# A graph-convolution and state-space kernel: the preparation of an item moved one slot up, and sums over channels taken by full products

## The chip, the cores and the metric

The kernel runs on one core of a Trainium2 chip. The core has a matmul engine (PE, with its weight loads shown apart as PEld), a vector engine (DVE), an activation engine (ACT), a general engine (POOL) and queues that issue DMA transfers (SP's is used here). The engines run side by side, each takes its own instructions strictly in the order of the program, and semaphores hold an instruction until its data and buffers are free. The metric is the device time of one execution in microseconds; the median of three runs counts.

## The reference, cut to what matters

The input is 16 images of 96 channels and 64 x 64 pixels. The first layer works in windows of 8 x 8 pixels: it finds each pixel's 9 nearest pixels of the window (by normalised channels), mixes pairs of pixels and takes the maximum. The second layer normalises each pixel over its channels and runs a state recurrence along the 4096 pixels, twice.

```python
# layer 0, per window of 64 pixels
y = affine(conv1x1(x, fc1_w, fc1_b), fc1_s, fc1_t)
xn = nodes / maximum(norm(nodes, axis=-1), 1e-12)          # sum of squares over 96 channels
idx = top_k(-(sq - 2 * xn @ xn.T + sq.T), 9)
h = max over k of gelu(affine(concat(x_i, x_j - x_i) @ ew + eb))
x = affine(conv1x1(h, fc2_w, fc2_b), fc2_s, fc2_t) + x
# layer 1, twice per image
h = (seq - mu) * rsqrt(var + 1e-5) * ln_g + ln_b           # mean and variance over 96 channels
xs, z = split(h @ in_w)
xc = silu(causal 4-tap convolution of xs)
dt, B, C = split(xc @ xproj_w)                             # 6, 16, 16 columns
delta = softplus(dt @ dt_w + dt_b)
state = exp(delta * A) * state + delta * B * xc            # 192 channels x 16 states
y = (sum over states of state * C + Dp * xc) * silu(z)
seq = seq + y @ out_w
```

At the end come a 1 x 1 convolution with a pooled term, a batch norm over all images and the residual.

## The kernel before, in words

**Rows and items.** The 4096 pixels of an image are 8 rows of windows, each 512 pixels. The first layer is done row by row: `nearest` (L288) finds the neighbours, `edges` (L360) the mixed pairs. The second layer is done in items (image, layer, row): 256 items, `n` from 0 to 255. Layer is `i` (0 or 1), row is `k`.

**Slots.** The main loop (L741) has one slot for each item `n` and each pair of states `p` from 0 to 7: 2048 slots, eight to an item. In a slot, for each of three blocks of 128 x 512, DVE makes `db` = u * B (`times_b`, L648) and runs the recurrence as a scan (L789). B comes from PE: `bcast` (L643) spreads two rows of `dbl` over 128 partitions into the PSUM tile `bt`, of which there is one buffer only. `bt` of the next slot is emitted in this slot, right after this slot's `db`s, and is read by the next slot's first `db`, which DVE takes ahead of this slot's third scan (L788). POOL multiplies the scans by C (`ct`, L803) and PE sums the products over the states (`folded`, L651: `ya` and `yb`); the sum of slot m - 1 is emitted at the end of slot m, behind everything else PE has in slot m, except in slot 0, where the sum of the old item's slot 7 comes ahead of it. ACT makes the decays `da` = exp(delta * A) for the slot after next (`chosen`, L626, called by `ahead`).

**Work between.** All other work is written as generators, each yielding once a slot. The loop keeps them in the list `going` and advances each by one step per slot, in the order of the list, between the first and the second scan. These are:

- `norm` (L509): the normalisation of an item; its sum over channels is `by_pixel` (L271): four products with one column each, 128 pixels per product.
- `prelude` (L540): the convolution and `z` with their silu (L567), then dt, B and C (`pd`, `dbl`), softplus (L590 to L613, ACT and POOL), and 16 DMAs that lay out delta and u.
- `nearest`: fc1, square, `by_pixel`, power, a trip through DRAM, scores, the eight largest, the indices to DRAM.
- `edges`: two halves; in each the indices come back, ACT makes one-hots (L384, L385), PE `pv` and ACT `vu`, then PE `t` and ACT gelu (L412); DVE takes maxima (L415, queued in `later`, and run between scans); `pf2` (L462) and the update of the row (L474).
- `tail` (L670): the out-projection of the item before, and for layer 1 the fusion product `po` and its statistics.

In the code's time, before the change, the steps of `prelude` for item n + 2 fall in slots 5, 6, (7), 0, 1, 2, 3, 4; `norm` for n + 3 in slots 7 to 4; gelu in slots 2 and 3; `tail` begins in slot 4. `nearest` and `edges` of a row begin in slot 5 of an odd item, so a row takes two items.

**PSUM.** All products of the generators share one ring `pm` of two buffers (tag `mm`): a product waits until the one two before it has been read. A step whose result DVE reads is split by `apart`: its products are emitted at the end of the steps of this slot (`close_steps`) and DVE's read at the start of the next slot's steps (`open_steps`).

**Tables.** Gelu and silu need another activation table than exp and ln. A generator that yields `TABLE` holds the loop off from calling `ahead` before the next slot's steps (`held`), so that the exps come after the burst.

Of the kernel before, what the change touches and what calls it, by code (L numbers as in the profile page):

```python
# [20 lines left out]
def tile_conv_knn_mamba(ctx: ExitStack, tc: tile.TileContext, w: dict, out: bass.AP):  # L21
# [107 lines left out]
    fc2_b, fc2_s, fc2_t = (column(f"fc2_{k}", f"L0_conv_fc2_{k}") for k in "bst")  # L129
    srow = load("fc2_srow", [128, C], w["L0_conv_fc2_s"].unsqueeze(0).to_broadcast([128, C]))  # L130
    nc.vector.tensor_tensor(fc2T, fc2T, srow.unsqueeze(1).to_broadcast([128, 3, C]), ALU.mult)

# [21 lines left out]
    )  # L154
    ones_c = const.tile([C, 1], F32, name="ones_c")
    nc.vector.memset(ones_c, 1.0)
    mhalf = const.tile([128, QJ], F32, name="mhalf")
# [87 lines left out]
    between = deque()  # L245
    later = []
    NDA = 12
# [19 lines left out]
    def open_steps():  # L267
        while opening:
            opening.pop(0)()

    def by_pixel(src, name):  # L271

        ps = pm.tile([128, QJ], F32, tag="mm", name=name)
        for j in range(QJ):
            nc.tensor.matmul(  # L275
                ps[:, j : j + 1],
                lhsT=src.rearrange("c (p j) -> c j p", j=QJ)[:, j, :],
                rhs=ones_c,
                start=True,
                stop=True,  # L280
            )
        return ps

# [4 lines left out]
    def nearest(b, q):  # L288
# [20 lines left out]
        nc.gpsimd.tensor_tensor(sq, y, y, ALU.mult)  # L309
        yield  # L310
        r4 = pr.tile([128, 2, QJ], F32, tag="r4", name=f"r4_{nm}")

        def clamped(ps):
            nc.vector.tensor_scalar(r4[:, 0], ps, 1e-24, None, ALU.max)
            nc.vector.tensor_copy(r4[:, 1], ps)

        apart(partial(by_pixel, sq, f"ss_{nm}"), clamped)
        yield

        nc.gpsimd.tensor_tensor(r4[:, 0], r4[:, 0], mhalf, ALU.pow)  # L320
        nc.gpsimd.tensor_tensor(r4[:, 1], r4[:, 1], r4[:, 0], ALU.mult)
# [7 lines left out]
        nc.sync.dma_start(out=hs[NN : NN + 1].rearrange("o w j -> o (w j)"), in_=r4_d[1:2, :])  # L329
        yield  # L330
        yield
# [28 lines left out]
    def edges(b, q):  # L360
# [3 lines left out]
        idx_d = chosen_of.pop((b, q))  # L364


        hqa = pr.tile([128, Q], F32, tag="hqa", name=f"hqa_{nm}", bufs=1)
        hqb = pr.tile([128, QH], F32, tag="hqb", name=f"hqb_{nm}", bufs=1)
        hqa4 = hqa.rearrange("p (r w c) -> p w r c", r=WS, w=NW)
        hqb4 = hqb.rearrange("p (r w c) -> p w r c", r=WS, w=NP)  # L370
        for hf in range(2):
# [4 lines left out]
            )  # L376
            yield
            yield
            vus = []
            for p in range(2):  # L380
                oh = ohs[p]

                ohj = oh[0:NN].rearrange("j w i k -> j w (i k)")
                nc.scalar.activation(ohj, idb[:, 2 * p : 2 * p + 2, :], AF.Abs, bias=minus_node)  # L384
                nc.scalar.activation(ohj, ohj, AF.Relu, bias=1.0, scale=-1.0)  # L385

                pv = pm.tile([128, 2, O], F32, tag="mm", name=f"pv_{nm}_{hf}_{p}")
                for h in range(2):
                    nodes = y[:, bass.ts(4 * hf + 2 * p + h, NN)]
                    nc.tensor.matmul(pv[0:NN, h, :], lhsT=nodes, rhs=ew2, start=True, stop=True)  # L390
                    nc.tensor.matmul(pv[NN:128, h, :], lhsT=nodes, rhs=ewd, start=True, stop=True)
                vu = pr.tile([128, 2, O], F32, tag="vu", name=f"vu_{nm}_{hf}_{p}")
                nc.scalar.copy(vu, pv)  # L393
                vus.append(vu)
                yield
            yield


            for p in range(2):
                ohw = [ohs[p][:, h].rearrange("j i k -> j (i k)") for h in range(2)]  # L400
                for part in range(3):
# [3 lines left out]
                    else:  # L405
# [7 lines left out]
                    w2 = 2 * hf + p  # L413
                    later.append(
                        partial(  # L415
# [34 lines left out]
            yield  # L450
            if hf == 0:
                yield
        yield
        yield
        nc.vector.tensor_tensor(hqa, hqa, sa, ALU.max)
        nc.vector.tensor_tensor(hqb, hqb, sb, ALU.max)
        yield
# [51 lines left out]
    def norm(n):  # L509

        b, i, k = items[n]
        nm = f"{b}_{i}_{k}"
        seq = seqs[b, k]
        hn = hns[n % NHN]
        if k == 0:
            nc.gpsimd.memset(hn[:, :HALO], 0.0)
        else:
            nc.gpsimd.tensor_copy(hn[:, :HALO], hns[(n - 1) % NHN][:, Q:])
        pc = pm.tile([C, Q], F32, tag="mm", name=f"pc_{nm}")
        nc.tensor.matmul(pc, lhsT=cmat, rhs=seq, start=True, stop=True)  # L520
        sq = pr.tile([C, Q], F32, tag="sq", name=f"sqv_{nm}")
        nc.scalar.activation(sq, pc, AF.Square)  # L522
        yield
        v4 = pr.tile([128, QJ], F32, tag="v4", name=f"v4_{nm}")
        apart(
            partial(by_pixel, sq, f"pvar_{nm}"),
            lambda ps: nc.vector.tensor_scalar(v4, ps, 1.0 / C, EPS, ALU.mult, ALU.add),
        )
        yield
        nc.gpsimd.tensor_tensor(v4, v4, mhalf, ALU.pow)  # L530
        yield
        rs_d = dram.tile([128, QJ], F32, tag="rs_d", name=f"rsd_{nm}")
        nc.sync.dma_start(out=rs_d, in_=v4)
        rs = pr.tile([C, Q], F32, tag="rs", name=f"rs_{nm}")
        nc.sync.dma_start(out=rs, in_=rs_d.rearrange("p j -> (p j)").unsqueeze(0).to_broadcast([C, Q]))
        yield
        yield
        nc.gpsimd.tensor_tensor(hn[:C, HALO:], seq, rs, ALU.mult)  # L538

    def prelude(n):  # L540
# [5 lines left out]
        xc = pr.tile([128, Q + QH], F32, tag="xc", name=f"xc_{nm}")  # L546
        z = pr.tile([128, Q + QH], F32, tag="z", name=f"z_{nm}", bufs=3)

# [26 lines left out]
        yield  # L575
        yield
        dbl = dbls[n % 2]
# [21 lines left out]
        for v, cols in ((va, slice(0, Q)), (vb, slice(Q, Q + QH))):  # L599
            nc.scalar.activation(e[:, cols], v, AF.Abs)  # L600
            nc.scalar.activation(rl[:, cols], v, AF.Relu)
        nc.scalar.activation(e, e, AF.Exp, scale=-1.0)
        s1 = pr.tile([128, Q + QH], F32, tag="s1", name=f"s1_{nm}", bufs=1)
# [47 lines left out]
    def folded(n, p, hb, y):  # L651

        i = items[n][1]
        xc = made[n][0]
        if p == 3:
            nc.tensor.matmul(y[0], lhsT=dp_diag[i][:, 0, :], rhs=xc[:, :Q], start=False, stop=False)
            nc.tensor.matmul(y[1], lhsT=dp_diag[i][:, 1, :], rhs=xc[:, Q:], start=False, stop=False)
        for h in range(2):
            nc.tensor.matmul(y[0][half(h)], lhsT=fold, rhs=hb[:, h, :], start=(p == 0), stop=(p == NPR - 1))  # L659
        for h in range(2):  # L660
            nc.tensor.matmul(  # L661
                y[1][half(h)], lhsT=fold, rhs=hb[:, 2, bass.ts(h, QH)], start=(p == 0), stop=(p == NPR - 1)
            )
# [6 lines left out]
    def tail(n):  # L670
# [17 lines left out]
        if i == NL - 1:  # L688
            yield
            yield  # L690
            yield
            po = pm.tile([C, Q], F32, tag="mm", name=f"po_{nm}")
            nc.tensor.matmul(po, lhsT=fusT[:, 0, :], rhs=seq, start=True, stop=True)
            o = pr.tile([C, Q], F32, tag="o", name=f"o_{nm}", bufs=1)
            nc.scalar.activation(o, po, AF.Identity, bias=gcs[b])
            yield
            nc.vector.bn_stats(stats[:, b * NQ + k, :], o)
            nc.sync.dma_start(out=o_d[b][:, bass.ts(k, Q)], in_=o)

    def drain(*several):  # L700

        several = list(several)
        while several:
            open_steps()
            several = [g for g in several if next(g, several) is not several]
            close_steps()
            while later:
                later.pop(0)()
        open_steps()
# [5 lines left out]
    for q in range(NQ):  # L715
        drain(*([nearest(0, q + 1)] if q + 1 < NQ else []), edges(0, q))
    for n in range(3):
        drain(norm(n))
        if n < 2:
            drain(prelude(n))  # L720

    AHEAD = 2
    order = [(n, p) for n in range(NI) for p in range(NPR)]
    coming = deque(order)
# [16 lines left out]
    for m, (n, p) in enumerate(order):  # L741
# [7 lines left out]
        if n > 1 and n % 2 == 1 and p == 5 and edge_row < NB * NQ:  # L749
            going.append(edges(*divmod(edge_row, NQ)))  # L750
            edge_row += 1
        between.extend(later)
        later.clear()
        if p == 0 and k == 0:
            state = pr.tile([128, NPR, NB3], F32, tag="state", name=f"state_{nm}")
        if p == 0 and i == 0 and k == 4:
            going.append(pooled(b))
        if p == 7 and n + 3 < NI:
            going.insert(0, norm(n + 3))
        if p == 5 and n + 2 < NI:  # L760
            going.insert(0, prelude(n + 2))
        ct, das = soon.pop((n, p))
# [6 lines left out]
        for c in range(NB3):  # L769
            if c == 1:  # L770
                if p == 1 and n:
                    gate(n - 1, y)
                if p == 4 and n:
                    going.append(tail(n - 1))
                open_steps()
                if not held:
                    ahead()
# [14 lines left out]
            if between and p not in (0, 1):  # L792
                between.popleft()()  # L793
        if p and behind is not None:
            if p == 1:
# [64 lines left out]
```

## Time and profile before

| | us |
|---|---|
| median of 3 runs (lowest, highest) | 14888.06 (14887.3, 14892.01) |
| the profiled execution's own time | 14897.12 |
| its span, first to last instruction | 14895.3 |
| setup, first image's rows, first items' preparation | up to 511 |
| main loop | 511 to 14611 |
| batch norm and output | 14614 to 14895 |

| engine | busy us | share of the span |
|---|---|---|
| PE | 13574.3 | 91% |
| DVE | 13114.8 | 88% |
| POOL | 10278.8 | 69% |
| ACT | 10114.4 | 68% |

| group | count | mean ns |
|---|---|---|
| scan L789, DVE | 6144 | 1269 and 1209 |
| `db` L648, DVE | 6144 | 680 |
| `hb` times C L803, POOL | 2048 | 3450 |
| `da` L637, ACT | 6144 | 710 |
| one-column products L275, PE | 3072 | 372 |
| their weight loads L275, PEld | 3072 | 327 to 330 |
| one-hots L384 and L385, ACT | 512 each | 1146 and 1057 |
| softplus L602, L604, L606, L607, ACT | 256 each | 845, 843, 844, 935 |
| power L530, POOL | 256 | 1018 |
| `rs` from DRAM, DMA | 256 | 3.4 us from issue to landing |
| table loads, ACT | 1024 | 1283 |

A profile is one execution. Busy time of PE is modelled from pipelined matmuls, so that a PE at 91% is not a PE at its peak; a matmul in fp32 appears as two instructions. The granted clock (PEclk) is the share of TensorE's full clock that its throttle let through; over the span it is 0.891. A row of a group gives shape, count, busy time, the mean of one and, behind the last bar, how long the engine sat idle before these instructions and what ended it.

### The profile page before, as it was taken

Reading aid. Unit: us, or ns where it says so; the run is one execution under the profiler, and the core shown is the slowest. Engines: PE = TensorE matmul, PEld = TensorE weight load, DVE = VectorE, ACT = ScalarE, POOL = GpSimd, SP = SyncE. Lnnn points to the kernel's source line nnn. Section 1 sums busy time; section 2 is a strip of 40 time slices with the busy share of each in tenths; the row PEclk is TensorE's granted clock in tenths of the full one; section 3 lists DMA queues with packets and bytes.
Section 4 is the critical chain, followed back from the end, with each engine's and each line's share of the span. In section 5 each row is a group of like instructions: output and inputs, shape, how many; then the busy total and the mean of one; then the engine's idle time right before and its main releaser. Section 6 shows DMA issues by size and latency. Waiting matters only on the chain. (4 is left out here: it accounts for less than half of the span.)

```text
span 14895.3 us, 168323 instructions
## 1 busy us (share of the span) xinstructions
PE 13574.3 (91%) x50248; PEld 5491.6 (37%) x50248; DVE 13114.8 (88%) x17401; ACT 10114.4 (68%) x14517; POOL 10278.8 (69%) x6279
## 2 busy tenths in 40 slices
PE   5799999999999999999999999999999999999982
PEld 2233333333333333333333333333333333333330
DVE  2699999999998999999999999999999999999984
ACT  4477777777777777777777777777777677677652
POOL 0577777777777777777777777777777777777771
PEclk8799899989998999999999999999999999989885
DMA  1233333333333333333333333333333333333337
GB/s 27 61 82 86 83 82 83 84 83 81 86 84 79 85 84 83 80 85 85 81 84 84 83 81 86 84 80 85 83 83 82 84 86 80 85 83 82 81 81 218
DMA packets 934023, 1256.95 MB, mean 84 GB/s; under 512 B 304672, under 2 KB 436142, under 8 KB 923888
## 3 DMA queue, kind: packets, MB, share of 16 engines
q1 hardware_dynamic: 929520, 1221.01, 31.7%
q10 hardware_dynamic: 3584, 25.17, 0.4%
q8 instruction: 396, 6.49, 0.2%
q14 instruction: 523, 4.28, 0.1%
HBM read 756.89 MB, written 85.98 MB: 57 GB/s over the span
## 5 line engine op out<-in xcount | busy, mean ns | idle before, releaser
L803 POOL TENSOR_TENSOR hb<-hb,ct 128x1536 f32<-128x1536 f32 x2048 | 7065.1, 3450 | 678.1 <-DVE hb L789 187.2
L789 DVE TENSOR_TENSOR_SCAN hb<-da,state,db 128x512 f32<-128x512 f32 x5376 | 6781.1, 1269 | 0.0
L648 DVE TENSOR_TENSOR db<-u,bt 128x512 f32<-128x512 f32 x6144 | 3992.1, 680 | 672.4 <-PE bt L643 670.3
L637 ACT ACTIVATE da<-delta,a 128x512 f32<-128x512 f32 x6144 | 3900.5, 710 | 61.6 <-DVE hb L789 48.6
L643 PE MATMUL bt<-dbl,bsel 39*128 39x512 f32 x4096 | 2466.0, 683 | 333.6 <-DVE db L648 330.3
L659 PE MATMUL ya<-hb,fold 128*64 128x512 f32 x8192 | 2424.8, 673 | 89.4 <-POOL hb L803 89.1
L802 POOL COPY state<-hb 128x3 f32<-128x3 f32 x1792 | 337.8, 189 | 2975.2 <-DVE hb L789 2550.8
L412 ACT ACTIVATE g<-t,eb,es 128x512 f32<-128x512 f32 x1536 | 1184.8, 777 | 1015.8 <-PE t L404 728.1
L567 ACT ACTIVATE xc<-pj,conv_b 128x512 f32<-128x512 f32 (+1 forms) x512 | 297.4, 581 | 1959.6 <-PE pj L555 1018.8
L661 PE MATMUL yb<-hb,fold 128*64 128x256 f32 x8192 | 1368.8, 415 | 0.0
L404 PE MATMUL t<-oh,vu 128*128 128x512 f32 x2048 | 1176.1, 700 | 45.7 <-ACT vu L393 29.4
L661 PEld LDWEIGHTS yb<-hb,fold 128*64 128x64 f32 x8192 | 640.5, 150 | 1359.0 <-issue 1358.7
L643 PEld LDWEIGHTS bt<-dbl,bsel 39*128 39x128 f32 x4096 | 659.4, 201 | 1164.1 <-DVE db L648 634.7
L555 PE MATMUL pj<-hn,conv_in 97*128 97x512 f32 x2048 | 953.0, 608 | 27.9 <-POOL hn L538 27.9
L789 DVE TENSOR_TENSOR_SCAN hb<-da,db 128x512 f32<-128x512 f32 x768 | 922.6, 1209 | 0.0
L659 PEld LDWEIGHTS ya<-hb,fold 128*64 128x64 f32 x8192 | 503.6, 145 | 1070.4 <-issue 726.9
L407 PE MATMUL t<-oh,vu 128*64 128x512 f32 x2048 | 583.7, 649 | 214.2 <-ACT g L412 209.2
L584 ACT COPY dbl<-pd 38x512 f32<-38x512 f32 x256 | 148.3, 579 | 855.9 <-PE pd L581 855.9
L404 PEld LDWEIGHTS t<-oh,vu 128*128 128x128 f32 x2048 | 386.2, 211 | 801.4 <-issue 521.4
L793 DVE TENSOR_REDUCE hqa<-g 128x64 f32<-128x512 f32 x960 | 634.1, 661 | 0.4 <-ACT g L412 0.3
L390 PE MATMUL pv<-ewT,y 96*64 96x192 f32 x2048 | 478.1, 361 | 124.7 <-ACT sqv L522 124.4
L384 ACT ACTIVATE oh<-idb,minus_node 64x1024 f32<-64x1024 uint16 x512 | 586.9, 1146 | 6.7 <-DMA idb<-idxd 6.7
(160 smaller groups left out, 18671.8 us busy)
## 6 DMA issues: line engine op xcount, KB each, us to landing
ct<-cd SPq DMA_DIRECT2D x4096, 128.0 KB, 3.0
delta<-ln SPq DMA_DIRECT2D x1024, 128.0 KB, 2.4
u<-s SPq DMA_DIRECT2D x1024, 128.0 KB, 2.3
idb<-idxd SPq DMA_DIRECT2D x256, 256.0 KB, 4.0
delta<-ln SPq DMA_DIRECT2D x1024, 64.0 KB, 2.0
u<-s SPq DMA_DIRECT2D x1024, 64.0 KB, 2.0
rs<-rsd SPq DMA_DIRECT2D x256, 192.0 KB, 3.4
x<-in_x SPq DMA_DIRECT2D x128, 192.0 KB, 4.5
```

The costliest lines, as they stand in the source:

```text
L384: nc.scalar.activation(ohj, idb[:, 2 * p : 2 * p + 2, :], AF.Abs, bias=minus_node)
L404: nc.tensor.matmul(t, lhsT=vus[p][:, part, :128], rhs=ohw[part], start=True, stop=True)
L412: nc.scalar.activation(g, t, AF.Gelu, bias=e_b[:, j : j + 1], scale=e_s[:, j : j + 1])
L555: nc.tensor.matmul(ps, lhsT=wt[:, t, :128], rhs=hn[:, off : off + Q], start=(t == 0), stop=(t == taps - 1))
L637: nc.scalar.activation(da, delta[:, c, :], AF.Exp, scale=a_neg[i][:, c, p : p + 1])
L643: nc.tensor.matmul(bt, lhsT=bsel[:, p, :], rhs=made[n][2], start=True, stop=True)
L648: nc.vector.tensor_tensor(db, made[n][5][:, c, :], bt, ALU.mult)
L659: nc.tensor.matmul(y[0][half(h)], lhsT=fold, rhs=hb[:, h, :], start=(p == 0), stop=(p == NPR - 1))
L661: nc.tensor.matmul(y[1][half(h)], lhsT=fold, rhs=hb[:, 2, bass.ts(h, QH)], start=(p == 0), stop=(p == NPR - 1))
L789: nc.vector.tensor_tensor_scan(hb[:, c, :], das[c], dbs[c], state[:, p, c : c + 1] if k else 0.0, ALU.mult, ALU.add)
L793: between.popleft()()
L803: nc.gpsimd.tensor_tensor(hb, hb, ct.unsqueeze(1).to_broadcast([128, NB3, Q]), ALU.mult)
```

## The change

It moves steps and replaces two reductions; the mathematics is the same.

- `norm` begins in slot 0 for item n + 2 (before: slot 7 for n + 3) and takes three slots. The variance is one product with a 96 x 96 matrix of ones, which leaves it on all 96 partitions at once; ACT takes Ln and Exp of it (exponent -0.5). `by_pixel`, the power on POOL and the trip through DRAM are gone.
- In `nearest` the sum of squares is one product with one column of ones as its weights (a result of 1 x 512), copied by ACT, written to DRAM and read back as 128 x 4; POOL clamps it.
- `prelude` begins in slot 4 and is appended to `going` behind what is there (before: slot 5, put in front): silu in slots 4 and 5, dt, B and C in 6, the first four softplus instructions in 7, the other four in 0, POOL's four in 1 and 2, the 16 DMAs in 3. `norm` is put in front of `going` in slot 0.
- In `edges` all four one-hot instructions of a half come in slot 6, ahead of both `pv`; the maxima go to DVE one slot later than before (slots 4 and 5 in place of 3 and 4), and those with `sa` and `sb` after the second scan of a slot; `pf2` comes in slot 1 and the row's update in slot 2 (before: slots 7 and 0).
- `tail` begins in slot 6; its fusion product is in slot 1 and its statistics in slot 3.
- `ahead` is called before the steps in slots 2 and 4 only, otherwise at the slot's end.
- The products with `Dp` come first in the sum over states (slot 1, with p = 0) and no longer with p = 3.
- `z` has four buffers in place of three; a scale row becomes a temporary tile, and `o` shares the tag of `xn`.

```diff
@@ nearest
-        def clamped(ps):
-            nc.vector.tensor_scalar(r4[:, 0], ps, 1e-24, None, ALU.max)
-            nc.vector.tensor_copy(r4[:, 1], ps)
-
-        apart(partial(by_pixel, sq, f"ss_{nm}"), clamped)
-        yield
-
+        ss = pm.tile([1, Q], F32, tag="mm", name=f"ss_{nm}")
+        nc.tensor.matmul(ss, lhsT=ones_cc[:, 0:1], rhs=sq, start=True, stop=True)
+        nc.scalar.copy(sq[0:1], ss)
+        ss_d = dram.tile([1, Q], F32, tag="ss_d", name=f"ssd_{nm}")
+        nc.sync.dma_start(out=ss_d, in_=sq[0:1])
         r4 = pr.tile([128, 2, QJ], F32, tag="r4", name=f"r4_{nm}")
+        nc.sync.dma_start(out=r4[:, 1], in_=ss_d.rearrange("o (p j) -> (o p) j", j=QJ))
+        yield
+        yield
+
+        nc.gpsimd.tensor_scalar(r4[:, 0], r4[:, 1], 1e-24, None, ALU.max)
         nc.gpsimd.tensor_tensor(r4[:, 0], r4[:, 0], mhalf, ALU.pow)
@@ edges
             yield
+            for p in range(2):
+                ohj = ohs[p][0:NN].rearrange("j w i k -> j w (i k)")
+                nc.scalar.activation(ohj, idb[:, 2 * p : 2 * p + 2, :], AF.Abs, bias=minus_node)
+                nc.scalar.activation(ohj, ohj, AF.Relu, bias=1.0, scale=-1.0)
             yield
             vus = []
             for p in range(2):
-                oh = ohs[p]
-                ohj = oh[0:NN].rearrange("j w i k -> j w (i k)")
-                nc.scalar.activation(ohj, idb[:, 2 * p : 2 * p + 2, :], AF.Abs, bias=minus_node)
-                nc.scalar.activation(ohj, ohj, AF.Relu, bias=1.0, scale=-1.0)
...
-                    later.append(
+                    later[1].append(
...
-            if hf == 0:
-                yield
-        yield
-        yield
-        nc.vector.tensor_tensor(hqa, hqa, sa, ALU.max)
-        nc.vector.tensor_tensor(hqb, hqb, sb, ALU.max)
+            yield
+        yield
+
+        late.append(partial(nc.vector.tensor_tensor, hqa, hqa, sa, ALU.max))
+        late.append(partial(nc.vector.tensor_tensor, hqb, hqb, sb, ALU.max))
+        yield
+        yield
         yield
@@ norm
         nc.scalar.activation(sq, pc, AF.Square)
         yield
-        v4 = pr.tile([128, QJ], F32, tag="v4", name=f"v4_{nm}")
-        apart(
-            partial(by_pixel, sq, f"pvar_{nm}"),
-            lambda ps: nc.vector.tensor_scalar(v4, ps, 1.0 / C, EPS, ALU.mult, ALU.add),
-        )
-        yield
-        nc.gpsimd.tensor_tensor(v4, v4, mhalf, ALU.pow)
-        yield
-        rs_d = dram.tile([128, QJ], F32, tag="rs_d", name=f"rsd_{nm}")
-        nc.sync.dma_start(out=rs_d, in_=v4)
+        ps = pm.tile([C, Q], F32, tag="mm", name=f"pvar_{nm}")
+        nc.tensor.matmul(ps, lhsT=ones_cc, rhs=sq, start=True, stop=True)
         rs = pr.tile([C, Q], F32, tag="rs", name=f"rs_{nm}")
-        nc.sync.dma_start(out=rs, in_=rs_d.rearrange("p j -> (p j)").unsqueeze(0).to_broadcast([C, Q]))
-        yield
+        nc.scalar.activation(rs, ps, AF.Ln, bias=eps_t[:C], scale=1.0 / C)
+        nc.scalar.activation(rs, rs, AF.Exp, scale=-0.5)
         yield
         nc.gpsimd.tensor_tensor(hn[:C, HALO:], seq, rs, ALU.mult)
@@ prelude
         nc.scalar.preload_act_table_set("natural_log_exp_and_others")
         yield
-        yield
         dbl = dbls[n % 2]
...
             nc.scalar.activation(rl[:, cols], v, AF.Relu)
+        yield
         nc.scalar.activation(e, e, AF.Exp, scale=-1.0)
@@ folded
-        if p == 3:
+        if p == 0:
...
@@ the main loop
-    for n in range(3):
+    for n in range(2):
         drain(norm(n))
-        if n < 2:
-            drain(prelude(n))
+        drain(prelude(n))
...
+    BURSTS = (2, 4)
...
-        between.extend(later)
-        later.clear()
+        between.extend(later[0])
+        later = [later[1], []]
...
-        if p == 7 and n + 3 < NI:
-            going.insert(0, norm(n + 3))
-        if p == 5 and n + 2 < NI:
-            going.insert(0, prelude(n + 2))
+        if p == 0 and n + 2 < NI:
+            going.insert(0, norm(n + 2))
+        if p == 4 and n + 2 < NI:
+            going.append(prelude(n + 2))
...
-                if p == 4 and n:
+                if p == 6 and n:
                     going.append(tail(n - 1))
                 open_steps()
-                if not held:
+                if p in BURSTS:
                     ahead()
...
+            while c == 1 and late:
+                late.pop(0)()
```

## The prediction

> **What bounds the kernel now.** First the page's busy times, then DVE's waits: DVE is the engine whose work cannot be moved, and the waits say who holds it up.
>
> ```profile
> PE 13574.3 (91%) x50248; PEld 5491.6 (37%) x50248; DVE 13114.8 (88%) x17401; ACT 10114.4 (68%) x14517; POOL 10278.8 (69%) x6279
> ```
> ```profile
> DVE db L648 <- PE bt L643: 670.3, 546, 12.3
> DVE x L474 <- PE pf L465: 314.0, 83, 5.2
> ...
> DVE v L527 <- PE pvar L275: 163.9, 144, 41.3
> ```
>
> Nearly all of it is PE being late, `bt` above all. The stretches view gives the main loop's sum, and eight of its slots: an even item's 0 to 2 and 6, the next odd item's 1 to 3 and 7 (columns: length, then busy time of PE, PEld, DVE, ACT, POOL; then PE's clock).
>
> ```profile
> 511.00:14611.00 14100.00, 13272.85 (x49247) 5371.68 (x49248) 12901.00 (x17045) 9794.06 (x14169) 10222.23 (x6215) 0.90 0.32 83
> ```
> ```profile
> 7136.49:7145.75 9.26, 9.26 (x37) 3.60 (x35) 6.57 (x9) 4.29 (x6) 4.51 (x4) 0.83 0.19 54
> 7145.75:7152.80 7.05, 6.75 (x26) 3.77 (x23) 6.23 (x11) 6.53 (x12) 4.66 (x4) 0.80 0.13 42
> 7152.80:7162.11 9.31, 9.31 (x21) 3.95 (x21) 5.48 (x10) 7.28 (x10) 8.08 (x8) 0.50 0.09 21
> ...
> 7182.84:7188.33 5.49, 5.49 (x31) 2.20 (x32) 5.24 (x8) 1.16 (x2) 4.86 (x4) 1.00 0.16 47
> ...
> 7201.18:7209.19 8.01, 8.00 (x28) 3.96 (x27) 7.25 (x17) 6.80 (x12) 4.67 (x4) 0.71 0.15 41
> 7209.19:7215.26 6.07, 4.97 (x14) 1.53 (x10) 5.42 (x8) 5.91 (x8) 5.35 (x3) 0.82 0.30 77
> 7215.26:7223.45 8.19, 7.01 (x26) 2.37 (x28) 7.18 (x10) 4.66 (x7) 8.03 (x5) 1.00 0.19 47
> ...
> 7244.07:7249.38 5.31, 5.17 (x8) 1.64 (x8) 5.31 (x8) 4.06 (x7) 3.77 (x4) 0.68 0.14 48
> ```
>
> DVE idles 14100 - 12901 = 1199 us in the loop, 4.68 an item; were all of it gone, the span would be 13696. Slots in which PE runs at full clock and ahead (6) are as long as DVE's work; the long ones have a low clock.
>
> **What lowers the clock.** The trace's clock record has two values, full and half; half-speed stretches in the loop last 3.4, 6.8, 10.2 or 13.7 us, rarely more, and begin on one grid of 3.413 us. PE just before such a stretch (it begins inside the `pdta` row, at 7149.9):
>
> ```profile
> 7146.63 2.03 PE L275 MATMUL pvar<-ones_c,sqv 96*128 96x1 f32 x8
> 7148.59 1.12 PE L643 MATMUL bt<-dbl,bsel 39*128 39x512 f32 x2
> 7149.55 1.53 PE L593 MATMUL pdta<-dbl,dt_w 39*128 39x512 f32 x2
> ```
>
> PE was never idle here. So I weighted every matmul's time by its rows of 128 (39 rows 0.30, 96 rows 0.75, one-column products nil) and summed it over each grid step. Of the full-speed steps of the loop, all below 1.35 us were followed by half speed, and none from 1.40 up; in half speed, no step below 2.5 us led back, every one above 2.75 did. I call this sum the weight.
>
> [...]
>
> **Edits, part by part.** Times in a slot are from the DVE's first `db` of it: two `db` 1.2, a scan 1.2, what DVE does between, a scan 1.2, then the next slot's first `db`, which needs `bt`: at 3.6 plus what lies between. A bare slot is 5.35 (5.31 in the last line above).
>
> DVE loses L527 (0.162) and half of L314 and L315 (0.156, 0.152, once in two items): **-0.32 an item**. POOL loses the power (1.02, L530) and gains a clamp at most like L321 (0.2, every other item): it is idle for 4604 us of the span, so nothing. Two DMAs an item go (2 KB, 192 KB), two per row come (2 KB each, 2.4 us to landing like `rsd`). SP then waits in slot 1 for ACT's copy and one landing, some 3 us, with the `ct` of two slots later behind it; cover is over 6 us: 0. The 16 layout DMAs move up a slot with what feeds them: more slack. POOL's four softplus products and L538 now fall in slots 1 and 2 (3.6 and 4.9 us beside 3.45 each), so that its product of slot 2 ends 3 us late; the fold that waits for it stands behind `t` in slot 3 and still leaves `bt` 1.2 to spare: 0, and a stall of what goes beyond that if slot 3 gets shorter. `z`'s fourth buffer, `o`'s tag, the temporary scale row: 0. ACT gains Ln and Exp (not shown at this shape; bounds 0.58, the 96x512 Square, and 0.84, the softplus Ln; I take 0.6 each) and the copy (0.58, L584, half). ACT's new sum of bursts is 6.7 us in slot 6 (one-hots 2 x 2.2, `dbl`, three exps), with two slots of lead for the exps: 0. What costs is where PE now waits. Three places:
>
> **Odd items, slot 7, into the even slot 0.** PE has `pd` and the out-projection in slot 6 (1.75 + 1.8, ended at 7.3 of 7.6), then waits 1.5 us for `db`, then `bt` (1.05) and `pdt` (1.65), all 39 rows, then 0.6 for Relu to free the buffer. Weight of a step that begins anywhere from 1.4 before slot 7 to 2.3 into it: 1.0 to 1.3. That is 3.7 us of starts, more than a step: it always falls. `pf`, `pv` and the fold then run at half speed, and `bt`, ready at 2.9 of slot 0 at full speed, comes at 4.6 to 7.3 by the phase, needed at 3.6: **2.3** (1.0 to 3.7; 0 if the clock holds).
>
> **Even items, slots 1 and 2.** In slot 0 `pc` follows the fold, which waits 3.7 us for POOL (L803, 3.45): it ends at 6.2, and ACT's Square, now in front of `going`, idles until then with softplus's tail (3.5, four rows) and `vu` (0.46) behind it. PSUM ring, in order: `pc`, `pv`, `pvar`, `ss`, (`po`), `pf2`. `ss` takes `pv`'s buffer, free after `vu`, 5.5 into slot 1; `pf2` takes that of `pvar`, free after ACT's three exps (1.93) and Ln, at 8.05 (layer 0), or of `ss` after Exp and copy, at 9.2 (layer 1). Behind `pf2` (1.9) stand the `Dp` products (1.4), the fold (1.45) and `bt` (1.05): 13.85 or 15.05 into slot 1, that is 7.5 or 8.7 into slot 2, against 4.9 with L474 and the row's mean between. Stall 2.6 or 3.8 at full speed. PE's two waits (1.9 and 1.5, around `ss`) give weights of 0.8 to 1.2: it falls again; half speed takes 1.5 to 2.6 of the work behind. **5.1** in the mean (2.6 to 6.4). `ss` itself, one row of output, no trace row: 0.74 (two 0.372 rows) to 1.02 (`pc`); I take 1.0, and inside the wait it hardly counts.
>
> **Odd items, slots 2 and 3.** The third `t` waits for a gelu to free its buffer. Today, in the odd item above, whose slot 3 begins with a `db` at 7214.08:
>
> ```profile
> 7214.30 1.28 ACT L412 ACT_TABLE_LOAD   x1
> ...
> 7216.43 1.08 PE L407 MATMUL t<-oh,vu 128*64 128x512 f32 x4 [2.26 <-ACT g L412]
> ```
>
> That is 2.35 into the slot. New: ACT's chain from Square, at 7.2 of slot 0 (PE is a little later than in the even item): 0.6 + 0.46 (`vu`) + 3.5 + 1.95 (exps) + 1.2 (Ln, Exp) + 0 or 0.7 (`o`, layer 1) + 2 x 1.95 + 1.28 (table) + 0.78 (gelu) ends 20.9 or 21.6 after slot 0 began; slot 3 begins at 18.9 (6.35 + 7.2 + 5.35): 2.0 or 2.7 into it. Then `t` 1.0, the fold 1.45, `bt` 1.05: 5.5 or 6.2, needed at 3.6 or 4.2, since the reductions that filled 1.2 of this slot are now in slots 4 and 5: 2.0 at full speed. PE's wait of over 3 us contains a step of low weight about 8 times in 10, and half speed then adds some 2.0: **3.6** (2.0 to 5.2).
>
> Even slots 3 and 4 (`ta` and `tb` come on top, 1.55): **0.6** (0.3 to 1.0). Slots 4 to 7 otherwise have `bt` in time: the convolution's 3.7 and 3.65 meet two reductions of 0.58 ahead of the need.
>
> **Sum.** Two items stall 2.3 + 5.1 + 0.6 + 3.6 = 11.6, one 5.8, against 4.68 now, with 0.32 less work: 0.80 x 240 items = +192. The last 16 items have no rows' work: their slots idle 5 us an item now (51.2 long, 46.2 busy), of which I leave 3: -38. Before the loop, the first two norms lose a trip through DRAM each (L538 waits 5.2 and 12.7 for it) and the third leaves; `nearest` gets one more, mostly beside `edges`: -25 (-40 to 0). 14895 + 129 = 15024 span; runs lie 7 us under the span, so **15017**.
>
> **Rivals.** *The clock stays up*: every step keeps 1.4, since the one-column products, in nearly every falling step today, are gone. Then the stalls at full speed are left, (0 + 3.2 + 0.3 + 2.0) / 2 = 2.75 an item: (2.75 - 4.68 - 0.32) x 240 - 63 = -603, 14285. For it: those products; against: the 39-row products and waits remain. The point is 5.26 us of stall an item, where the sum is nought: one fall that doesn't happen (2.3, 1.9 or 1.6 in two items) is enough. *Falls at one place only*, or ACT ahead by more than I see: stalls near 4.0, -240 - 63: 14585. *Every fall in its worst phase*: (3.7 + 6.4 + 1.0 + 5.2) / 2 = 8.15: +756 - 63, 15581. *It does nothing*: low weight moves from slot 1 to 7 and stalls equal today's within 0.2 an item: 14888 +- 30.
>
> **Numbers.** 0.2% is 30 us, about what a measurement here can tell from none. Forecast (slower, 14918 to 15330) 0.49; worst phase 0.07; nothing 0.06; one place 0.25; clock up 0.13. Slower 0.56, same 0.06, faster 0.38. Likeliest alone 14918 to 15330; the range reaches 14400 to 15350.
>
> **What would show it.** Right: half-speed stretches begin in odd slot 7 and even slot 1, even slots 0 and 2 the longest, `pf` L462 waiting on ACT, `bt` still DVE's first releaser. Wrong: mean clock above 0.95; DVE idle under 1000 us in the loop; `ss` starting before `vu` ends; or half speed beginning in slots 2 to 4 of the odd items alone.

## The result, and the profile after

The changed kernel takes 14952.44 us (median of 6 runs, 14945.4 to 14960.82); the kernel before, beside it on the same chip, takes 14890.03 (14884.06 to 14899.54). The ratio is 1.0041, with a 95% interval of 1.0028 to 1.0054. So it is slower, as forecast, but by 62 us and not by 129.

The page's busy times of the changed kernel:

```profile
span 14943.6 us, 163112 instructions
PE 13020.1 (87%) x47944; PEld 4708.2 (32%) x47944; DVE 12888.8 (86%) x16889; ACT 10545.5 (71%) x15157; POOL 10056.7 (67%) x6151
```

PE has 554 us less to do and DVE 226 us less, and the span is 48 us longer. The waits of DVE, then those of ACT and PE that matter here (the columns: time in all, times, the longest):

```profile
DVE db L634 <- PE bt L629: 1098.1, 526, 47.5
DVE x L468 <- PE pf L459: 415.7, 126, 4.7
```
```profile
ACT sqv L516 <- PE pc L514: 752.0, 254, 7.2
```
```profile
PE ss L303 <- ACT vu L379: 209.1, 119, 1.8
...
PE pf L456 <- ACT rs L521: 75.9, 58, 1.3
```

`bt` is still what DVE waits for first. New is ACT's wait at Square: 752 us, where the kernel before has 16.1 at its own Square. The stretches view gives the whole loop, then one even item's slots 0 to 2 (layer 1) and an odd item's 2 and 3, each from a slot's first scan to the next slot's (columns as before: length, busy time of PE, PEld, DVE, ACT, POOL, then PE's clock):

```profile
516.80:14664.70 14147.90, 12712.77 (x47012) 4600.50 (x47012) 12680.21 (x16554) 10216.80 (x14797) 10003.37 (x6081) 0.93 0.30 79
7274.80:7283.24 8.44, 8.44 (x37) 3.19 (x36) 5.42 (x8) 3.60 (x7) 4.74 (x5) 0.77 0.00 0
7283.24:7289.48 6.24, 3.36 (x10) 0.65 (x6) 6.24 (x10) 6.09 (x10) 5.20 (x3) 0.95 0.00 0
7289.48:7302.27 12.79, 12.59 (x32) 5.04 (x34) 6.86 (x10) 8.43 (x13) 10.44 (x8) 0.76 0.45 109
...
7346.93:7352.24 5.31, 3.04 (x6) 0.97 (x6) 5.31 (x8) 5.29 (x9) 5.23 (x4) 1.00 0.00 0
7352.24:7361.56 9.32, 8.12 (x24) 2.63 (x26) 6.01 (x9) 4.13 (x6) 8.49 (x7) 0.82 0.44 105
```

DVE idles 14147.9 - 12680.2 = 1468 us in the loop, where it idled 1199: +269. It works 12680.2 where it worked 12901.0: -221. The sum, +48, is the whole difference of the spans. The long slots are even 0 and 2 and odd 3 (means over items 17 to 239: 7.8, 11.6 and 9.2 us); even slot 1 and odd slot 2 show PE half idle right before the last two.

ACT at the start of that even item, from its timeline (start, time, what, and in brackets the idle time before it):

```profile
7277.42 1.95 ACT L623 ACTIVATE da<-delta,a 128x512 f32<-128x512 f32 x3
7282.74 0.59 ACT L516 ACTIVATE sqv<-pc 96x512 f32<-96x512 f32 x1 [3.37 <-PE pc L514]
7283.23 0.83 ACT L588 ACTIVATE e<-e 128x768 f32<-128x768 f32 x1
...
7286.74 0.46 ACT L379 COPY vu<-pv 128x384 f32<-128x384 f32 x1
```

Square waits 3.4 us for `pc`, and softplus's tail and `vu`, which want nothing from `pc`, wait with it.

A fall is the beginning of a half-speed stretch in the clock's record. Falls counted over items 17 to 239 by their slot: before, even slot 1 (111 times), odd slot 1 (112) and odd slot 7 (70). After, odd slot 7 or even slot 0 (54 + 57), even slot 1 or 2 (69 + 42) and odd slot 2 or 3 (39 + 73): one fall in each pair of items at each of the three places that the prediction names.

### The profile page after: what moved, and what is told of

The parts are those of the page before. It is cut to its first block, busy times and chain, and to the rows that moved or that the text cites. A ratio compares the mean times of both kernels' runs of the same rounds, so it can differ in the third digit from the quotient of the medians.

```text
span 14943.6 us, 163112 instructions
## 1 busy us (share of the span) xinstructions
PE 13020.1 (87%) x47944; PEld 4708.2 (32%) x47944; DVE 12888.8 (86%) x16889; ACT 10545.5 (71%) x15157; POOL 10056.7 (67%) x6151
## 5 line engine op out<-in xcount | busy, mean ns | idle before, releaser
L629 PE MATMUL bt<-dbl,bsel 39*128 39x512 f32 x4096 | 2365.0, 658 | 358.1 <-DVE db L634 356.3
L647 PE MATMUL yb<-hb,fold 128*64 128x256 f32 x8192 | 1333.4, 406 | 0.0
L397 PE MATMUL t<-oh,vu 128*128 128x512 f32 x2048 | 1120.0, 672 | 59.8 <-ACT g L405 46.7
L629 PEld LDWEIGHTS bt<-dbl,bsel 39*128 39x128 f32 x4096 | 628.2, 192 | 1232.1 <-DVE db L634 692.3
L595 POOL TENSOR_TENSOR e<-e,s 128x768 f32<-128x768 f32 x256 | 465.6, 1819 | 355.4 <-ACT s L593 355.4
L516 ACT ACTIVATE sqv<-pc 96x512 f32<-96x512 f32 x256 | 151.9, 593 | 752.0 <-PE pc L514 752.0
```

The costliest lines, as they stand in the source:

```text
L397: nc.tensor.matmul(t, lhsT=vus[p][:, part, :128], rhs=ohw[part], start=True, stop=True)
L629: nc.tensor.matmul(bt, lhsT=bsel[:, p, :], rhs=made[n][2], start=True, stop=True)
L647: nc.tensor.matmul(y[1][half(h)], lhsT=fold, rhs=hb[:, 2, bass.ts(h, QH)], start=False, stop=(p == NPR - 1))
```

## The experiments

Fifteen runs in four series, each series on one chip beside the kernel before. "DVE" is its busy time in an item and "stall" its idle time in gaps of over 0.15 us, means over items 17 to 239, worked out from the trace; "clock" is the granted clock of the profiled execution. A point is one hundredth of the time of the kernel before.

| run | median us | ratio [95%] | DVE | stall | clock |
|---|---|---|---|---|---|
| before (profile) | 14888 | 1 | 50.87 | 4.47 | 0.891 |
| after (profile) | 14952 | 1.0041 [1.0028, 1.0054] | 49.94 | 5.48 | 0.914 |
| e1 before, maxima late | 14973 | 1.0091 [1.0074, 1.0108] | 50.32 | 5.28 | 0.885 |
| e2 after, maxima in place | 14983 | 1.0094 [1.0077, 1.0111] | 50.31 | 5.25 | 0.909 |
| e3 after, 128 rows | 14748 | 0.9935 [0.9918, 0.9951] | 49.90 | 4.83 | 0.928 |
| e4 before, 128 rows | 14771 | 0.9949 [0.9931, 0.9966] | 50.85 | 4.15 | 0.927 |
| e5 after again | 14949 | 1.0055 [1.0038, 1.0072] | 49.94 | 5.48 | 0.913 |
| e6 after, norm last | 14094 | 0.9481 [0.9465, 0.9497] | 49.85 | 2.03 | 0.933 |
| e7 e6 and 128 rows | 14018 | 0.9429 [0.9413, 0.9445] | 49.81 | 1.93 | 0.949 |
| e8 after, one maximum twice | 14996 | 1.0085 [1.0068, 1.0102] | 50.28 | 5.26 | 0.909 |
| e9 after, Square alone last | 14448 | 0.9720 [0.9704, 0.9736] | 49.87 | 3.52 | 0.917 |
| e10 before, norm last | 15518 | 1.0437 [1.0419, 1.0454] | 50.99 | 7.05 | 0.862 |
| e11 after, old norm | 14405 | 0.9692 [0.9676, 0.9708] | 49.99 | 3.03 | 0.906 |
| e12 e6, tail in slot 7 | 14966 | 1.0069 [1.0053, 1.0086] | 50.00 | 5.61 | 0.899 |
| e14 after, norm in slot 7 | 14902 | 0.9973 [0.9963, 0.9982] | 49.97 | 5.17 | 0.901 |
| e15 e14 and 128 rows | 14531 | 0.9725 [0.9709, 0.9741] | 49.94 | 3.92 | 0.937 |
| e16 e6, maxima in place | 14089 | 0.9434 [0.9418, 0.9449] | 50.23 | 1.65 | 0.934 |

The kernel before itself had medians of 14845, 14868, 14861 and 14942 in the four series (chips), 0.65% apart, so that ratios of two series may differ by as much with nothing behind it; the changed kernel's own times on two chips (14952 and 14949) stand closer than their ratios. Small differences across series are therefore given both ways below.

**The maxima.** The diff queues the maxima of `hqa` with `sa` and `hqb` with `sb` in `late`. The rows of the first one, before and after:

```profile
L455 DVE TENSOR_TENSOR hqa<-hqa,sa 128x512 f32<-128x512 f32 x128 | 244.3, 1909 | 0.0
```
```profile
L782 DVE TENSOR_TENSOR hqa<-hqa,sa 128x512 f32<-128x512 f32 x120 | 80.0, 667 | 0.0
```

1.24 us less, once in two items. In the kernel before it stands beside POOL's product:

```profile
7237.64 2.04 DVE L455 TENSOR_TENSOR hqa<-hqa,sa 128x512 f32<-128x512 f32 x1
```
```profile
7235.68 3.44 POOL L803 TENSOR_TENSOR hb<-hb,ct 128x1536 f32<-128x1536 f32 x1
```

POOL ends at 7239.12, the maximum at 7239.68. Of the 128, 120 overlap a POOL product, take 1.84 to 2.05 us and end 0.544 to 0.558 us after POOL does; the other 8 take 0.68. After the second scan POOL's product has ended, and all 128 take 0.66 to 0.68. The 120 end 0.55 us after POOL's product, whenever they began, and not 0.68 after their own start: I read what is over 0.68 as a wait for that product. The trace counts it as busy time (2.04 us in the row above).

e1 gives the kernel before this one edit, e2 takes it out of the changed kernel (the reverse of the lines below):

```diff
-        nc.vector.tensor_tensor(hqa, hqa, sa, ALU.max)
-        nc.vector.tensor_tensor(hqb, hqb, sb, ALU.max)
+        late.append(partial(nc.vector.tensor_tensor, hqa, hqa, sa, ALU.max))
+        late.append(partial(nc.vector.tensor_tensor, hqb, hqb, sb, ALU.max))
```

> The kernel before, with one part of the change alone: the two maxima with sa and sb go to DVE after the second scan of slot 6 instead of ahead of it. In the trace before, the larger one takes 1.9 us and ends 0.55 us after POOL's product that runs beside it; after the change it takes 0.67. Sum theory (time is DVE's work plus the stalls, each on its own): 0.62 us an item less, -159 us, ratio 0.989. Lock theory (both traces have image loops of 260 or 261 whole steps of the clock gate's 3.413 us grid, so the loop falls into step with the grid and small savings turn into waiting): images of a whole number of steps again, 258 to 260, ratio 0.994 to 1.000.

> The changed kernel with that part undone: the two maxima ahead of the second scan. Sum theory: +159 us against the changed kernel, ratio to before 1.015. Lock theory: whole steps an image, 260 to 262, ratio 1.004 to 1.009.

e1: DVE's work fell by 0.55 us an item and the stall rose by 0.81: slower, against both theories, and its images are not whole steps (259.2 to 266.0). e2: 1.38 us a maximum, 0.37 us of work more in an item, 0.23 us of stall less. It is 35 us slower than e5, the unaltered kernel on another chip, or 58 by the two ratios; its images are at 261.0 steps, and its ratio of 1.0094 is at the upper end of the lock theory's range and far from the sum theory's 1.015.

e5 and e8 ran on one chip with e6 and e7. e8 queues `hqa`'s maximum twice, so that nothing but DVE's work is altered.

> The changed kernel again, nothing altered, on the chip of this series, beside the kernel before. Sum theory (each kernel's time is its DVE work and its stalls, wherever it runs): ratio 1.004 again, 1.002 to 1.007, and the stall of an item 5.3 to 5.7 us. Step theory (an image of 16 items settles on a whole number of the clock's 3.413 us steps, and on which of several depends on where the loop starts on that grid): the images are whole numbers of steps again, 260 or 261, but the ratio can be anything from 1.000 to 1.009.

> The changed kernel with the maximum of hqa and sa done twice, both after the second scan: 0.67 us more of DVE's work in two items, nothing else altered. Sum theory: 0.33 us an item, 80 us in the loop, ratio 1.009 to 1.011 if the unaltered kernel is at 1.004. Step theory: images stay at whole steps, 260, 261 or 262 each, so the time is that of the unaltered kernel plus 0, 51 or 102 us.

e5 repeats 14952 within 4 us. In e8 DVE's work rose by 0.34 us an item and the stall fell by 0.22; the time rose by 47 us, 11 of them ahead of the loop, where 80 of work were added. So DVE's time does not add up on its own here: within these items two thirds are given back as less stall. The step theory forecast images of whole steps, and from the second on all are at 261.0, where those of e5 are at 260 or 261. PE catching up while DVE is busy would look the same; no run parts the two.

**The rows.** e3 and e4 pad `bt`'s and dt's products from 39 to 128 rows, with zeros in the weights (`bsel`, `dt_w`) and ones in `dbl`, in the changed kernel and in the one before:

```diff
-    bsel = const.tile([R + 2 * NS + 1, NPR, 128], F32, name="bsel")
+    bsel = const.tile([128, NPR, 128], F32, name="bsel")
...
```

> The changed kernel with the 39-row products (bt and the dt products) padded to 128 rows: zero weights, ones in the other operand, same results. Fall theory (a step of the grid with under 1.36 us of matmul time weighted by rows brings half speed): hardly any half speed in the loop, clock above 0.97 there, DVE's stall from 5.5 to about 2.75 us an item, -700 us, ratio to before 0.957. Rival (the gate counts idle time, not rows): clock 0.91 and time of the changed kernel, ratio 1.004.

> The kernel before with the same padding; the one-column products stay. Fall theory: bt and the dt products beside the one-column ones now give a step 1.4 us and more, so few falls, clock above 0.97, stall from 4.5 to some 2 us an item, -600 us, ratio 0.96. Rivals: the one-column products alone bring half speed (clock 0.89, ratio 1.00); or the gate counts idle time (the same).

`bt`'s rows in the changed kernel and in e3:

```profile
L629 PE MATMUL bt<-dbl,bsel 39*128 39x512 f32 x4096 | 2365.0, 658 | 358.1 <-DVE db L634 356.3
```
```profile
L630 PE MATMUL bt<-dbl,bsel 128*128 128x512 f32 x4096 | 2375.2, 662 | 450.9 <-DVE db L635 445.8
```

The same products at nearly the same length, and in both kernels the clock rises: half speed in the loop, from its first scan to its last, falls from 2098 to 1649 us and from 2769 to 1704. So rows count for the clock, though the rows that were added multiply by zero. But both runs came out between their theory (0.957 and 0.96, a clock above 0.97) and their rivals (1.004 and 1.00): the stalls of even slot 2 (4.8 and 5.1 by layer) and odd slot 3 (3.0 and 2.7) hardly move in e3. So these two do not come from few rows alone.

**The wait at Square.** e6 changes one call: norm no longer goes ahead of the other steps in slot 0. As `going` keeps its order, norm's later steps come behind the others too: in even items PE takes `pv` ahead of `pc` in slot 0 and `ss` ahead of `pvar` in slot 1.

```diff
-            going.insert(0, norm(n + 2))
+            going.append(norm(n + 2))
```

> The changed kernel with the next norm put behind the other work of slot 0 and not in front of it, so that Square no longer holds up softplus's tail and vu on ACT. Stall theory (the stalls of even slot 2 and odd slot 3 come from ACT's chain being late, as predicted): even slot 2 falls from 4.3 to 5.2 us to 1 to 2, odd slot 3 from 3.5 to 0.5 to 1.5, the idle time of DVE per item from 5.5 to about 3, so some 600 us less: ratio 0.965, 0.955 to 0.975. Rival (PE's low weight, not ACT, makes the falls, and one fall is as good as another): half speed moves to other slots, ratio 0.99 to 1.005.

> The edit of the run before, and the products with 39 rows padded to 128 rows with zeros. If the two causes (late ACT, few rows) add up: another 0.01 to 0.02 below the run before, 0.94 to 0.96, and a granted clock over 0.95. If they are one and the same fall: within 0.005 of the better of the two single ones.

It is 5.2% under the kernel before, more than expected. The same three slots of an even item in e6, and the odd item's 2 and 3:

```profile
6854.56:6862.16 7.60, 7.60 (x36) 2.95 (x32) 5.42 (x8) 6.77 (x10) 4.78 (x5) 0.78 0.00 0
6862.16:6868.40 6.24, 6.21 (x16) 2.14 (x16) 6.24 (x10) 5.55 (x10) 6.16 (x3) 1.00 0.05 7
6868.40:6875.08 6.68, 6.67 (x24) 2.32 (x24) 6.65 (x10) 5.95 (x9) 6.52 (x5) 1.00 0.34 105
...
6919.74:6925.44 5.70, 4.78 (x17) 1.63 (x18) 5.42 (x7) 5.67 (x9) 5.62 (x3) 1.00 0.00 0
6925.44:6931.70 6.26, 6.25 (x24) 2.05 (x24) 6.01 (x9) 2.77 (x4) 6.10 (x6) 1.00 0.65 155
```

Even slot 2 is 6.68 us long and not 12.79, slot 1's PE is busy and not half idle, the clock full. Over items 17 to 239 the stall of even slot 2 goes from 4.3 and 5.2 (layers 0 and 1) to 0.0 and 0.1, that of odd slots 2 and 3 together from 3.6 and 3.4 to 1.65 and 0.9; even slot 0 keeps its stall (2.7 in both layers, 2.3 and 2.7 without the edit). Nearly all falls are of two kinds, each once in two items: odd slot 1 (111 times) and odd slot 7 or even slot 0 (112). And ACT goes straight through:

```profile
6860.24 0.94 ACT L593 ACTIVATE s<-s,neg 128x768 f32<-128x768 f32 x1
6861.29 0.48 ACT L379 COPY vu<-pv 128x384 f32<-128x384 f32 x1
6862.31 0.59 ACT L516 ACTIVATE sqv<-pc 96x512 f32<-96x512 f32 x1 [0.54 <-PE pc L514]
```

e7 adds the 128 rows: 0.005 more, the fastest version of the study, 14018 us. In e5 to e3 the rows were worth 12 thousandths (1.0055 to 0.9935, on two chips); so most of what they save seems to be the same time.

e9 leaves `pc` where it is and moves Square alone (the diff below); e10 makes e6's edit in the kernel before, whose norm is in slot 7.

```diff
-        nc.scalar.activation(sq, pc, AF.Square)
+        squares.append(partial(nc.scalar.activation, sq, pc, AF.Square))
...
                 going = still
+                while squares:
+                    squares.pop(0)()
```

> The changed kernel with nothing moved but Square itself: pc stays the first product of slot 0 on PE, and with it the order of the PSUM buffers; only on ACT does Square go behind the rest of the slot (softplus's Exp to Identity, vu). Theory (ACT's 2.85 us of waiting at Square, with softplus's tail and vu behind it, makes the stalls of even slot 2 and odd slot 3): the same gain as with the whole norm behind, ratio 0.948, 0.94 to 0.96. Rival (the order of PE's products and of the PSUM buffers makes them): 0.99 to 1.006.

> The kernel before with its norm put behind the other work of slot 7, the same edit as in the changed kernel. Theory (ACT's wait at Square came with the change: in the kernel before pc is free to run in slot 7, and Square shows no wait there): ratio 0.993 to 1.007. Rival (the order is worth the same in either kernel): 0.94 to 0.965.

e9 lies between its two theories. From e5 (1.0055) to e6 (0.9481) are 0.057; ACT's order alone gives 0.034 of it (501 of 855 us by the times, on two chips). In e9 the stall of even slot 2 is down to 0.4 and 0.5, so Square's place on ACT makes that one. Odd slots 2 and 3 together keep 3.3 and 3.0, now in slot 2: their gain in e6 comes with the order of PE's products and of the PSUM buffers, which no run altered alone. In e9 PE waits longer for Square in slot 1 than in e6:

```profile
PE pvar L520 <- ACT sqv L777: 391.6, 120, 3.5
```
```profile
PE pvar L519 <- ACT sqv L516: 189.7, 122, 3.2
```

(e9 first, then e6.) e10 contradicts both theories: the edit that is worth -5.7 points in the changed kernel costs 4.4% in the one before. Falls begin there in odd slot 0 (56 times) and even slot 0 (28), where that kernel has none, and ACT waits longer for `pd`, the product that gives dt, B and C (first the kernel before, then e10):

```profile
ACT dbl L584 <- PE pd L581: 855.9, 256, 6.5
```
```profile
ACT dbl L584 <- PE pd L581: 1296.8, 256, 7.9
```

Whether that wait makes the loss no run shows.

e11 puts the norm of the kernel before into the changed one (slot 7, one-column products); e14 begins the new norm in slot 7, e15 with 128 rows as well.

> The changed kernel with the norm of the kernel before: it begins in slot 7, one item earlier, with the one-column products and the trip through DRAM, and one empty step fewer. Theory (Square's place in slot 0 is what costs; in slot 7 it waits for nothing): the stalls of even slot 2 and odd slot 3 shrink, the one-column products bring a fall into slot 0 or 1 in their place: ratio 0.965 to 0.99. Rival (leaving out the one-column products is what the change gains by): 1.01 to 1.03.

> The changed kernel with its norm (Ln and Exp, no one-column products) begun in slot 7, one slot earlier and first there, as in the kernel before. Theory (Square in slot 7 waits for nothing, so ACT's wait in slot 0 goes as in the run at 0.948; and pc's 0.77 of weight lifts slot 7's 1.0 to 1.3 over the 1.4 at which no fall was seen, so the odd items' fall in slot 7 goes too): stall of even slot 0 under 0.7 us, ratio 0.92 to 0.935. Rival (the fall comes from PE's wait for Relu, or is only moved): even slot 0 still stalls over 2 us, ratio 0.943 to 0.96.

> The run before with the products of 39 rows padded to 128 rows with zeros as well. Theory: another 0.002 to 0.01 below it, and a clock over 0.97 if no fall is left but those where PE truly waits. Rival (falls follow PE's waits, not its rows): within 0.003 of it.

e11 came as expected: with the one-column products, the power on POOL and the trip through DRAM back, it is 3.6 points faster than the change as it is (544 us by the times). Its norm leaves nothing on ACT in slot 0. e14 missed. `pc` moved, but now `pvar` is the product in slot 0 behind the fold, and Ln the first on ACT behind it:

```profile
ACT rs L521 <- PE pvar L519: 741.5, 255, 6.4
```

741.5 us against Square's 752.0: the wait belongs to the place, not to the instruction. In e14 odd slot 7 falls still begin (98 in 112), so `pc`'s weight was not enough there, or not in the right step. e15 is 2.5 points under e14, more than its theory's 0.2 to 1.0 and against its rival, with the clock at 0.937 and not over 0.97: here the rows are worth twice the 1.2 points of e5 to e3.

e12, on e6, moves the out-projection into slot 7 to fill it:

```diff
-                if p == 6 and n:
+                if p == 7 and n:
                     going.append(tail(n - 1))
```

> The changed kernel with the norm behind the other work of slot 0, as in the run at 0.948, and the out-projection one slot later, in slot 7, where the odd items' clock falls. Theory (the fall from odd slot 7 into even slot 0 comes from the low weight of slot 7, bt and pdt of 39 rows alone; 1.8 us of 128-row products fill it): even slot 0's stall of 2.7 us goes to under 0.7, 1.0 to 1.35 us an item, ratio 0.925 to 0.935. Rival (those products only push pf, pv and the fold of slot 0 later): 0.945 to 0.96.

A miss: it takes away the whole gain. The edit made a wait of its own: DVE's update of the row, taken ahead of slot 0's steps, now waits for the product:

```profile
DVE x L672 <- PE pow L667: 985.6, 243, 7.2
```

> The version at 0.948 (norm behind the other work of slot 0) with the maxima of hqa and hqb left where the kernel before has them. Sum theory (the move of the maxima is worth the time that they take off DVE, 0.7 us in two items): 83 us, ratio 0.951 to 0.957. Rival (that time is PE's to catch up in, and is given back as stall): 0.946 to 0.950.

e16 undoes the move of the maxima in e6: 14089 against 14094, on two chips. DVE works 0.38 us more in an item and idles 0.38 less: by the times the move is worth nothing there. The ratio, 0.9434 for 0.9481, lies under both forecasts, but the kernel before took longer on that chip (runs of 14889 to 14955).

## Why the prediction was half right

**The places of the stalls: right.** Odd slot 7 into even slot 0, even slots 1 and 2, odd slots 2 and 3: each has one fall in each pair of items. `ss` waits for `vu`, and behind it `pf2` in layer 0 and `po` in layer 1 wait for Ln (L521), as worked out from the PSUM ring. Measured against forecast: even slot 0 2.3 and 2.7 (2.3), even slot 2 4.3 and 5.2 (5.1), even slot 4 0.35 and 0.15 (0.6 in slots 3 and 4), odd slot 3 3.6 and 3.4 (3.6). One of its signs failed: odd slot 3 (9.2 us) is longer than even slot 0 (7.8). That Square's wait makes the stall of even slot 2 is what e9 shows; for odd slot 3 it is not shown, as moving Square alone left a stall of that size one slot earlier.

**The stall's size: right.** +1.12 us an item was forecast, 269 us in 240 items; in these DVE's idle time grew by 255, 1.06 an item. That the whole loop's idle time grew by 269 is luck: on the last 16 items a gain of 38 us was forecast, and they became 11 us longer (818.1 to 829.4, with 16 more idle).

**DVE's work: the step that failed.** The prediction has "DVE loses L527 (0.162) and half of L314 and L315 (0.156, 0.152, once in two items): **-0.32 an item**", -77 us. Measured: -0.93 an item, -221 us in the loop. The maxima that the change moves behind the second scan stand in its sum at nothing, without a reason, and L455 is not looked at. Its row had 1909 ns, where `db` of the same shape takes 680: the sign that it waits inside. Putting it behind the second scan takes 1.24 us off, 0.62 an item; that and 0.32 is the 0.93. The term is 144 us off, the difference of the spans is 81 us off (48 for 129). What lies between came out the other way: before the loop -25 was forecast and its first scan began 4 us later (500.5 for 496.9), and the last 16 items were 49 us off.

**What the term is worth.** Not its 144 us. Undoing the move costs 35 us in the changed kernel by the times of e2 and e5, 58 by their ratios, and nothing in e6 by the times; the 80 us of e8 cost 47. Without the move (e2) the change stands 138 us over the kernel before on the same chip (14983 and 14845), or 95 over the 14888 of the prediction: nearer to 129 than the 62 measured, either way. The prediction adds up work and stall as if they were apart; where DVE waits for PE in the same item they are not (e2, e8).

**The clock rule: right, and it holds elsewhere.** Counted over the loops of all seventeen profiles, with each one's own phase of the 3.413 us grid: of 5226 full-speed steps with a weight under 1.35 us, 5221 were followed by half speed (the other five, all in e4, weigh 1.33 to 1.35); of 52804 with 1.5 or more, 181 were, none of them over 1.72. Between 1.35 and 1.5 it goes both ways, so "none from 1.40 up" holds for the kernel before and is too sharp for the others. PE's busy time without the rows does much worse: at its best threshold 3148 of the 58926 steps stand on the wrong side, with the weight 460. And e3 and e4 raise the clock by rows alone (0.914 to 0.928 and 0.891 to 0.927), where the rivals by which idle time counts had 0.91 and 0.89.

**Rival "the clock stays up".** Its point was that the one-column products caused the falls. They stand right before the fall that the prediction shows, but e4 keeps them and loses over a third of the half-speed time, and e11, which has norm's back, beats the change.

**What stays open.** Even slot 0's stall: it was laid to the low weight of odd slot 7, and neither e12 nor e14 filled that slot without a new wait. Why e10 loses 4.4%. And why taking DVE time off the kernel before (e1) made it slower: with the kernel before, not even the sign of the move's worth came out as the sum has it.

## What to carry to other kernels

When a step is moved to the head of a slot, ask what the first instruction on each in-order engine waits for, and what stands behind it that does not: here putting a norm behind the five ACT instructions and the products that need nothing from it gave 5.7 points, 3.4 of them by ACT's order alone, though in e10 the same edit cost 4.4% in another schedule. A mean far over that of its like (here 1909 ns for 680) can be a wait inside the instruction, and moving it moves time. Work taken off the engine that bounds a slot is only gained where it does not wait in the same stretch anyway: count both, and test a term by doubling it.

## What the runs showed of the hardware

**Whole steps.** In ten of the seventeen profiles the time of an image of 16 items settles on a whole number of the clock's 3.413 us steps. In units of the step, from the third image on: 260.0 in all images before; 260.0 or 261.0 after and in e5; 261.0 in e2 and e8, whose edits differ; 257 in e3 (but for two images), 259.0 in e14, 253.0 in e15, 249.0 in e11, 250 or 251 in e9. In before, after, e2, e14 and e15 the starts of the images then keep their phase on the grid within some 0.1 us. One step per image is 16 x 3.413 = 55 us, of the size of what e2 and e8 cost. That the loop stretches until it meets the grid, so that a small edit can vanish or cost a whole step, is how I read it; it isn't shown. The others are not so bound: e10 is often at 271 or 273 but not always, e1 (259.2 to 266.0), e4 (256.7 to 260.0), e7 (242.2 to 244.0), e12 (258.9 to 263.1), e6 and e16 (243.0 to 244.4) spread, some with as many stalls as the change.

**A maximum held by POOL.** The maximum of `hqa` and `sa`, which both lie in SBUF, takes 0.67 us alone and up to 2.05 beside POOL's product, then always ending 0.55 after it (120 times in the kernel before, 120 in e2). Scans and `db` read one tile from SBUF and one from PSUM (`db` and `bt` lie there), and run beside POOL's product at their usual length: in the kernel before 1.268 us for a scan inside it and 1.269 outside, 0.683 and 0.681 for `db`. Whether it is the operands' place that makes the difference is not shown: no run altered it.
